# Expert slots that are given out 0.7 of a step later from the fourth group on

## The chip, the cores and the metric

The kernel runs on one core of a Trainium2 chip. The metric is the time of one execution on the device in microseconds (us). Before the change four runs gave 1210.75 to 1219.62 us, with a median of 1216.89 us.

## What is computed

The input is four images of 256 channels and 64 x 64 pixels, in 32-bit floats. Layer 0 is a local attention (each pixel looks at its 3 x 3 neighbours) behind a group norm and an instance norm. Layer 1 treats each pixel as a token: a windowed attention over 64 tokens, then a mixture of eight experts in which every token goes to two of them.

```python
# layer 0
x = x + _L0_conv_ref(_gn(x), ...)
# layer 1: tokens
t = _to_tokens(x)
t = t + _L1_attn_ref(_ln_t(t), Wp, bp, Wg)
t = t + _L1_ffn_ref(_ln_t(t), router_w, w1, b1, w2, b2)
...
    rw, re = jax.lax.top_k(probs, 2)
    for e in range(8):
        h = gelu(tokens @ w1[e] + b1[e])
        out = out + combine[:, e:e + 1] * (h @ w2[e] + b2[e])
```

## The kernel before

**Blocks and steps.** The 16,384 tokens are cut into NB = 32 blocks of 512. The main loop runs over steps g = 0 to 33. A step works on several blocks at once, each at another stage: attend(g) is the second half of the local attention, tail(g-1) the windowed attention and the router of the block before, ranks(g-2) finds the place of every token of the block before that in its expert's list, and produce(g+1) starts the next block. These four are generators. The loop goes round them and takes one piece of each in turn. A step has about 27 pieces, and after each of them follow(g + n/27) is called.

**Rows.** For each of a block's four tiles of 128 tokens and each of a token's two choices, ranks queues one indirect transfer that scatters the rows to the DRAM buffer `rows_in` by expert (L1001, on POOL's queue, 256 in all). They wait in the list `waiting` until give_rows hands them out: two or four with each slot's sum, and all that are left of a group just before a slot of that group is fetched.

**Groups and slots.** The first 28 blocks form 15 groups: 13 of two blocks and two of one. (The last four blocks are handled apart, in `halves` and `together`.) When a group's last block has been ranked, the group's slots are known: a slot is 256 rows of one expert. There are 105 slots. Group 0 has 1, the groups of two have 8 each, the groups of one have 4 each, so `first_slot` is 0, 1, 9, 17, ..., 97, 101, 105.

**One slot** (generator `experts`): a fetch of 272 KB from `rows_in` on SP's queue (L1171, tile sx, 8 buffers); a copy of the expert's first weights on ACT (L1188); four transposes on PE (L1195) and a copy of their result on ACT (L1199); eight matmuls (L1207), and two Gelu on ACT (L1213); eight matmuls (L1225), and two additions and two products on DVE (L1229, L1230); two indirect transfers on POOL's queue that add the rows to `out` (L1244). The parts of one slot are spread over the generator's turns: a slot is fetched two slots ahead of its transposes. Each slot takes four turns.

**What sets the order.** follow(at) decides how many turns of `experts` stand behind each piece of the blocks' work. It takes the smaller of two broken lines over the step number `at`. `most` says how many slots may have been given out: it passes through the points (begins[k], first_slot[k] - 3), where begins[k] is the moment at which the first slot of group k may be fetched. `wanted` is a straight line that spreads the slots evenly: from 1 slot at 6.35 to 94 at step 32, which is 3.63 slots a step. Where `most` is the smaller, eight slots go to two steps, so 4 a step.

The framework that lowers the program keeps close to this order, though it can put an instruction earlier: the first fetch (L1171) is issued at 121.9 us, in step 4, while the lines ask for the first slot after 6.35.

**Ramp and end.** Before step 4 no rows are there, so there are no slots. For blocks below RAMP = 7 the token rows are scaled on ACT, later on DVE. The last four blocks' experts run behind step 33, in smaller units.

Of the kernel before, what the change touches and what calls it, by code (L numbers as in the profile page):

```python
# [62 lines left out]
def hybrid_block_kernel(ctx: ExitStack, tc: tile.TileContext, ins: dict, out: bass.AP):  # L63
# [29 lines left out]
    NS = NB - 4  # L93
    GROUPS = (*[2] * 13, *[1] * 2)
    assert sum(GROUPS) == NS
    first_of = [sum(GROUPS[:k]) for k in range(len(GROUPS))]
# [1361 lines left out]


    STEPS, LAG = {NB: 17, NB + 1: 12}, 0.35  # L1460
    begins = [at + 2 + LAG for n, at in enumerate(first_of[1:])] + [NS + 2.0]
    most = [(at, max(0, n - FETCH - 1)) for at, n in zip((*begins, NB + 2.0), (*first_slot, first_slot[-1]))]
    wanted = [(begins[1], 1), *((NB + n, first_slot[-1] - m) for n, m in ((0, 11), (1, 7), (2, 3)))]
    stream, done = experts(), 0
# [17 lines left out]
    for g in range(NB + 2):  # L1482
# [10 lines left out]
        n = 0  # L1493
# [75 lines left out]
```

## Time and profile before

| | |
|---|---|
| runs | 1210.75 to 1219.62 us, median 1216.89 |
| profiled execution, its own time | 1213.42 us |
| its span, first to last instruction | 1211.7 us |
| TensorE clock granted, mean | 0.975 |
| DVE busy | 916.5 us, 76% |
| ACT busy | 856.6 us, 71% |
| POOL busy | 702.4 us, 58% |

A block's step is taken here to end with the second of its two sums after the output projection (L738, DVE). In the timeline these ends lie at:

| step | ends at, us | length, us |
|---|---|---|
| 5 | 158.0 | 25.2 |
| 6 | 185.3 | 27.3 |
| 7 | 212.6 | 27.3 |
| 8 | 242.4 | 29.8 |
| 9 | 275.1 | 32.7 |
| 12 | 373.4 | 32.8 (mean of steps 9 to 12) |
| 14 | 441.1 | |
| 20 | 631.2 | 31.7 (mean of steps 15 to 20) |
| 22 | 695.6 | |
| 29 | 919.3 | 32.0 (mean of steps 23 to 29) |
| 31 | 977.5 | |

Steps 13 and 21 (38.2 and 35.7 us) also hold the norm of a new image.

PE is TensorE's matmuls and PEld its weight loads, DVE is VectorE, ACT ScalarE, POOL GpSimd, SP SyncE, which issues the plain DMAs. "PE 32.70 (x263)" in a view by windows reads: busy for 32.70 us in this stretch, with 263 matmul instructions. In a list of waits, each line has the engine and line that waited, what it waited for, and then the total in us, how often, and the longest.

### The profile page before, as it was taken

What the parts mean: (1) busy time and instruction counts of PE and PEld (TensorE: products, weight loads), DVE (VectorE), ACT (ScalarE), POOL (GpSimd) and SP (SyncE); (2) the same over time, 40 slices, a digit from 0 to 9 for tenths busy, and PEclk for the clock granted to TensorE, in tenths of its full rate; (3) what the DMA queues carried; (4) which work ended last, traced back from release to release, by engine and by line L of the source; (5) the groups of instructions that cost most, each with busy time, mean ns of one, the idle gap of its engine ahead of it and who ended that gap; (6) DMA issues with size and microseconds to landing.
All of it is one profiled execution on the core that took longest, in us unless ns stands there. A gap on an engine that the chain in (4) does not pass through costs nothing. (4 is left out here: it accounts for less than half of the span.)

```text
span 1211.7 us, 29026 instructions
## 1 busy us (share of the span) xinstructions
PE 1108.0 (91%) x8762; PEld 791.9 (65%) x8762; DVE 916.5 (76%) x4632; ACT 856.6 (71%) x1752; POOL 702.4 (58%) x642
## 2 busy tenths in 40 slices
PE   5989889999999999999999999999999999868890
PEld 4545456677776766776677766766766677757780
DVE  4588878888898888888888887888878889324344
ACT  1466769788888788777787787877787766436660
POOL 3114226566665667566664756666565767577772
PEclk9999999999999999999999999999999999979995
DMA  9885547776768677777676777677665445845556
GB/s 286 270 305 175 177 136 239 207 177 164 185 178 182 167 210 184 187 201 207 164 174 153 181 188 174 176 175 172 150 167 122 100 104 113 198 88 127 139 124 238
DMA packets 136145, 214.00 MB, mean 177 GB/s; under 512 B 16368, under 2 KB 102400, under 8 KB 131768
## 3 DMA queue, kind: packets, MB, share of 16 engines
q1 hardware_dynamic: 86264, 137.00, 37.2%
q0 software_dynamic: 48352, 73.05, 29.3%
q10 hardware_dynamic: 1376, 2.10, 0.5%
q8 instruction: 73, 1.20, 0.4%
q14 instruction: 80, 0.66, 0.2%
HBM read 120.78 MB, written 91.31 MB: 175 GB/s over the span
## 5 line engine op out<-in xcount | busy, mean ns | idle before, releaser
L1244 POOL DMA_INDIRECT out<-sx x210 | 335.3, 1597 | 212.8 <-issue 40.3
L1001 POOL DMA_INDIRECT rows_in<-tok,rows x256 | 254.7, 995 | 185.6 <-issue 71.6
L1225 PE MATMUL psy<-w,h 128*128 x840 | 213.3, 385 | 0.8 <-issue 0.8
L1207 PE MATMUL psh<-xc,w1s 128*128 128x256 f32 x840 | 204.7, 385 | 0.0
L1225 PEld LDWEIGHTS psy<-w,h 128*128 128x128 f32 x840 | 152.7, 190 | 51.3 <-issue 26.2
L1207 PEld LDWEIGHTS psh<-xc,w1s 128*128 128x128 f32 x840 | 152.5, 191 | 34.5 <-issue 10.4
L576 PE MATMUL psq<-x,qks 128*128 128x512 f32 x256 | 125.4, 612 | 1.8 <-ACT qks L497 1.8
L734 PE MATMUL pso<-mixT,vo 128*128 128x512 f32 x256 | 123.4, 605 | 0.0
L1229 DVE TENSOR_TENSOR sx<-psy,b2b 128x256 f32<-128x256 f32 x210 | 87.7, 418 | 45.8 <-PE psy L1225 41.0
L1213 ACT ACTIVATE h<-psh,w1s 128x256 f32<-128x256 f32 x210 | 88.2, 472 | 31.0 <-PE psh L1207 30.1
L1199 ACT COPY xc<-ptx 128x512 f32<-128x512 f32 x105 | 61.2, 583 | 27.1 <-PE ptx L1195 26.6
L1230 DVE TENSOR_SCALAR sx<-sx 128x256 f32<-128x256 f32 x210 | 77.0, 367 | 2.1 <-DVE sx L1229 0.2
L1213 ACT ACT_TABLE_LOAD x59 | 75.7, 1283 | 0.8
L893 ACT ACTIVATE x<-x,scale 128x256 f32<-128x256 f32 x120 | 63.2, 591 | 18.2 <-DVE scale L867 17.6
L584 ACT ACTIVATE q<-psq,qbb,irc 128x512 f32<-128x512 f32 x64 | 50.0, 781 | 34.4 <-PE psq L576 27.9
L1195 PE MATMUL ptx<-ident,sx 128*128 128x128 f32 x420 | 65.2, 277 | 7.6 <-DMA sx<-rows_in 7.6
L1195 PEld LDWEIGHTS ptx<-ident,sx 128*128 128x128 f32 x420 | 50.5, 144 | 32.4 <-issue 15.9
L780 PE MATMUL psp<-wpr,x1c 128*128 128x136 f32 x512 | 70.3, 282 | 0.4 <-DVE ispread L473 0.4
L576 PEld LDWEIGHTS psq<-x,qks 128*128 128x128 f32 x256 | 46.2, 195 | 35.6 <-issue 34.6
L780 PEld LDWEIGHTS psp<-wpr,x1c 128*128 128x128 f32 x512 | 65.6, 190 | 4.5 <-issue 2.1
L734 PEld LDWEIGHTS pso<-mixT,vo 128*128 128x128 f32 x256 | 45.5, 190 | 34.3 <-issue 30.1
L832 PE MATMUL psw<-wl,bandl 128*64 128x512 f32 x128 | 67.0, 635 | 0.0
(277 smaller groups left out, 2501.2 us busy)
## 6 DMA issues: line engine op xcount, KB each, us to landing
xp<-in_xp SPq DMA_DIRECT2D x32, 1024.0 KB
sx<-rows_in SPq DMA_DIRECT2D x105, 272.0 KB
x<-in_x SPq DMA_DIRECT2D x32, 660.0 KB
xs<-in_xs SPq DMA_DIRECT2D x32, 512.0 KB
out<-x SPq DMA_DIRECT2D x28, 512.0 KB
sxa<-rows_in SPq DMA_DIRECT2D x32, 136.0 KB
rows_in<-tok,rows POOLq DMA_INDIRECT x256
out<-sx POOLq DMA_INDIRECT x210
```

The costliest lines, as they stand in the source:

```text
L576: inst = nc.tensor.matmul(ps.rearrange("p (r w) -> p r w", w=W), qks[:, ci, co * P : (co + 1) * P], t[:, ci, 1 : TH + 1, 1 : W + 1], start ...
L734: nc.tensor.matmul(ps, vo[:, ci, co * P : (co + 1) * P], mixT[:, ci, :], start=(ci == 0), stop=(ci == NC - 1),)
L780: nc.tensor.matmul(ps[:, u, :], xc[:, ci, t * P : (t + 1) * P], wpr[:, ci, :], start=(ci == 0), stop=(ci == NC - 1),)
L832: one = nc.tensor.matmul(to[0:WIN], bandl, wl[part], start=True, stop=True)
L1001: return nc.gpsimd.indirect_dma_start(out=rows_in[:, :], out_offset=bass.IndirectOffsetOnAxis(ap=rows[:, c, t : t + 1], axis=0), in_=tok[: ...
L1195: nc.tensor.transpose(pt[:, c, t * P : (t + 1) * P], xs[:, t, c * P : (c + 1) * P], ident)
L1207: nc.tensor.matmul(ps[:, f, :], w1s[:, o : o + P], xc[:, ci, :], start=(ci == 0), stop=(ci == NC - 1),)
L1213: inst = nc.scalar.activation(h[:, f, :], ps[:, f, :], AF.Gelu, bias=w1s[:, F1 + f : F1 + f + 1])
L1225: nc.tensor.matmul(ps, h[:, f, t * P : (t + 1) * P], w2[:, e, f, :], start=(f == 0), stop=(f == NC - 1),)
L1229: nc.vector.tensor_add(ys[:, t, :], ps, b2b[:, e, :])
L1230: nc.vector.tensor_scalar_mul(ys[:, t, :], ys[:, t, :], xs[:, t, bass.ds(e + C, 1)])
L1244: inst = nc.gpsimd.indirect_dma_start(out=out, out_offset=bass.IndirectOffsetOnAxis(ap=xs[:, t, C + E : C + E + 1].bitcast(U32), axis=0), ...
```

## The change

`begins` is computed in another way. Nothing else is touched.

```diff
     STEPS, LAG = {NB: 17, NB + 1: 12}, 0.35
-    begins = [at + 2 + LAG for n, at in enumerate(first_of[1:])] + [NS + 2.0]
+    begins = [at + 2 + min(LAG * max(n, 1), 1.05) for n, at in enumerate(first_of[1:])] + [NS + 3.0]
     most = [(at, max(0, n - FETCH - 1)) for at, n in zip((*begins, NB + 2.0), (*first_slot, first_slot[-1]))]
     wanted = [(begins[1], 1), *((NB + n, first_slot[-1] - m) for n, m in ((0, 11), (1, 7), (2, 3)))]
```

first_of[k] is the first block of group k: 0, 2, 4, ..., 24, 26, 27. The points of `most` move as follows:

| group | first fetch, step, before | after |
|---|---|---|
| 0 | 4.35 | 4.35 |
| 1 | 6.35 | 6.35 |
| 2 | 8.35 | 8.70 |
| 3 | 10.35 | 11.05 |
| 4 | 12.35 | 13.05 |
| 5 to 12 | 14.35 to 28.35 | 0.70 later each |
| 13 | 29.35 | 30.05 |
| 14 | 30.0 | 31.0 |

`wanted` starts at begins[1], which is 6.35 in both.

## The prediction

> **What bounds the kernel now.** I read the page first: its sums, then PE in 40 slices of some 30 us each, about one slice to a step.
>
> ```profile
> PE 1108.0 (91%) x8762; PEld 791.9 (65%) x8762; DVE 916.5 (76%) x4632; ACT 856.6 (71%) x1752; POOL 702.4 (58%) x642
> ...
> PE   5989889999999999999999999999999999868890
> ```
>
> PE has no slack in the middle. The windows by step say where it has some: steps "4 and 5" together, then 6, 7 and 8 alone, then three long stretches without an image norm.
>
> ```profile
> 109.00:158.00 49.00, 40.25 (x394) 22.78 (x394) 41.15 (x258) 32.27 (x74) 17.47 (x22) 0.93 0.53 171
> 158.00:185.30 27.30, 23.32 (x207) 14.90 (x208) 19.77 (x124) 19.68 (x42) 8.73 (x10) 0.94 0.42 141
> 185.30:212.60 27.30, 26.46 (x228) 17.51 (x227) 24.51 (x145) 26.97 (x52) 16.16 (x16) 1.00 0.83 250
> 212.60:242.40 29.80, 29.80 (x248) 20.70 (x247) 25.10 (x126) 23.68 (x50) 16.65 (x14) 1.00 0.75 205
> 242.40:373.40 131.00, 130.82 (x1042) 93.85 (x1041) 111.92 (x564) 110.16 (x207) 83.06 (x69) 1.00 0.70 176
> 441.10:631.20 190.10, 188.59 (x1517) 132.05 (x1516) 162.11 (x831) 151.38 (x294) 124.00 (x103) 1.00 0.75 192
> 695.60:919.30 223.70, 222.06 (x1780) 155.72 (x1779) 184.52 (x983) 174.99 (x343) 141.18 (x117) 1.00 0.69 172
> ```
>
> The columns after the length are PE, PEld, DVE, ACT, POOL, then the clock. In step 6 PE is idle for 4.0 us, in step 7 for 0.8 (there ACT is busy for 26.97 of 27.3 us), and from step 8 on for less than 1% of the time. So from step 8 on the end is set by the sum of PE's work, and the order of the work costs only what it makes PE wait.
>
> What a slot costs PE I take from starts, as busy times overlap. The timeline of PE in step 8 to 9 has a whole slot's three parts in a row:
>
> ```profile
> 241.47 0.60 PE L1195 MATMUL ptx<-ident,sx 128*128 128x128 f32 x4
> 241.91 1.89 PE L1207 MATMUL psh<-xc,w1s 128*128 128x256 f32 x8
> 243.64 1.89 PE L1225 MATMUL psy<-w,h 128*128 x8
> 245.36 0.60 PE L1195 MATMUL ptx<-ident,sx 128*128 128x128 f32 x4
> ```
>
> From 241.47 to 245.36 is 3.89 us a slot. The first stretch (steps 9 to 12) holds 128 of the eight-a-slot matmuls L1225, so 16 slots: 131.0 - 16 x 3.89 = 68.8, or 17.2 us a step for the blocks' own work. Steps 15 to 20 hold 176, so 22 slots: 190.1 - 85.6 = 104.5, or 17.4 a step. Steps 23 to 29 hold 208, so 26: 223.7 - 101.1 = 122.6, or 17.5 a step. Four slots to every step is 0.2 to 0.3 us a step better than an uneven 3.6 or 3.7.
>
> Last, the waits of SP for scattered rows, because that is what an early fetch must meet. The first line below is of the list of SP's waits from 213 to 412 us, the second from 412 to 700, the third of SP's timeline.
>
> ```profile
> SPq L1171 <- DMA rows_in<-tok,rows: 45.1, 4, 17.3
> ...
> SPq L1171 <- DMA rows_in<-tok,rows: 29.4, 4, 14.0
> ...
> 250.85 13.45 SPq L1171 DMA_DIRECT2D sx<-rows_in  x3
> ```
>
> From 700 to 978 us there is no such wait. SP stands for 74.5 us, but PE doesn't: its waits for sx between 133 and 978 us are 4.8 us in all, and both lie before 213.
>
> **What the change moves.** No instruction is added or removed. Putting numbers into the two lines of the code, the slots due are:
>
> at step 7: 1.95 before, 1.66 after; at 8: 4.95, 4.21; at 9: 8.60, 7.02; at 10: 12.60, 10.43; at 11: 16.60, 13.83; from 11.05 to 14.35 2.80 fewer; at 17: 39.61, 37.80; at 20: 50.49, 49.80; from 22 on the same.
>
> Before, `most` is the lower line until 14.35, at 4 slots a step, and `wanted` after it at 3.63. After, `most` rules until about 21.7: 2.55 slots a step up to 8.70, 3.40 up to 11.05, then 4. The last points (31.0 for 30.0) never decide: at 30 `wanted` is 86.75 and `most` 94 or more. So the change is this: up to 2.80 slots are taken out of steps 6 to 10 and put back in steps 14 to 21. Groups 0 and 1 start as before, and the last ten steps and the end behind step 33 get the same order.
>
> **Step by step.** A moved slot takes everything along. PE: 3.89 us. ACT: the weights' copy 0.627, the copy of the transposes 0.583, two Gelu of 0.472, and 12 table loads of 1.283 in the 16 slots of 242 to 373 us, 0.96 each; 3.1 us in all. DVE: 2 x (0.418 + 0.367) = 1.57. POOL: two sums of 1.597 and the up to four row transfers of 0.995 that it hands out. SP: the fetch (272 KB, 0.38 us to issue). On SP's queue the fetch falls behind the loads of x, of the patches and of the statistics and the store of that part of the step, which thus go earlier; on POOL's the sums and rows fall behind the rim copies (0.84).
>
> 1. Slots leave step 6: 0.29 x 3.89 = 1.1 us of PE work. Step 6 is not set by PE (23.32 of 27.3), so I refund nothing: +1.1. The bounds: 0, if it shortens by as much, and 0.74 x 3.89 = 2.9, if step 7, which loses 0.45 slot more, doesn't shorten either. I take 1.1, as step 7 is full on ACT and 0.45 x 3.1 us of that leave too.
> 2. Slots leave steps 8 to 10: 2.77 - 0.74 = 2.03 slots. PE is full there, so they shorten by 2.03 x 3.89 = 7.9, as long as nothing else becomes the limit. DVE is the next: 25.10 of 29.8 in step 8, less 0.84 x 1.57. With 2.9 slots step 8 would have 17.2 + 11.3 = 28.5 against 23.8 on DVE: it stays PE's. An uneven 3.4 costs 0.25 a step more: +0.75.
> 3. The 2.8 slots come back in steps 14 to 21, 10.9 us, which cancels the 7.9 and what left steps 6 and 7. Eight steps go to an even 4: 8 x -0.25 = -2.0. The bounds of this evenness: 0, if it is chance, and the ceiling worked out in the first rival.
> 4. The fetch of a group's first slots comes 0.7 step, some 23 us, after the old place; the longest wait for rows was 17.3 us. So most of SP's 74.5 us vanish. What hides them now is the lead of two slots (half a step, 16 us) between fetch and transposes, with PE waiting for none of it after 213 us. I cost it at 0. What SP meets next is its wait for a free sx buffer (140.8 us from 412 to 700), which PE doesn't see either. If the cover failed, one late fetch would cost PE up to 17.3 - 16 = 1.3 us, eight of them 10.
>
> Sum: 1.1 + 0.75 - 2.0 + 0 = -0.2 us on the profiled execution's 1213.4 (its span is 1211.7, with 1.7 outside). That one lies 3.5 us under the median of the runs, 1216.9; so about 1216.5 for the median.
>
> [...] The view of PE in step 6 has this:
>
> ```profile
> 164.79 2.12 PE L780 MATMUL psp<-wpr,x1c 128*128 128x136 f32 x16
> 170.84 0.33 PE L1195 MATMUL ptx<-ident,sx 128*128 128x128 f32 x1 [3.93 <-DMA sx<-rows_in]
> 171.01 3.00 PE L576 MATMUL psq<-x,qks 128*128 128x512 f32 x4
> ```
>
> After 3.93 us without work four matmuls took 3.00 us that take 1.89 at 252.97, and the step's clock was 0.94: 0.06 x 27.3 = 1.6 us lost. From 185 us to 887 the clock is 1.00. [...]
>
> **The rivals.**
>
> *Faster: the middle has hidden waits, and the early fetches made them.* The blocks' own PE work in step 9, start to start, is 16.4 us (psw 2.0, ptp 0.2, ptx 0.9, psq 3.5, psr 0.6, psc 1.0, psp 1.9, ptm 0.9, psk 0.4, pss and psb 1.4, pso 3.5). Against 17.2 to 17.5 that leaves 0.8 to 1.1 us a step that could go, 15 us over steps 8 to 22, and 4.8 in steps 6 and 7. If half of the 15 went, it would be -7.5: 1209. For: SP's 74.5 us of waits sit in exactly these steps, and hold back the loads queued behind. Against: steps 23 to 29, which have none of these waits, are no better (17.5).
>
> *Slower: the ramp has a floor.* If steps 6 to 10 are held by the blocks' own chain of stages and not by PE, removing slots returns nothing, and they are paid in full later: 2.77 x 3.89 = 10.8, so up to 1227.7; with two thirds, about 1224. It decides from 1.6 slots on that aren't refunded (6.1 us). For: steps without any slot still take 24.5 us (49.0 for two), and three-slot steps later 30.2 to 30.5. Against: PE is busy for all of step 8's 29.80.
>
> *It doesn't do what it says.* If the framework reorders by readiness, the new points hardly move the instructions, and the time is 1216.9.
>
> **How the numbers follow.** About 0.5% (6 us) is what a measurement of this kernel can tell from no change. No difference beyond that, my forecast with the third rival in it: 0.46, its own range 1211 to 1222. Faster 0.26, at 1204 to 1210. Slower 0.28, at 1223 to 1230. The likeliest is 1216.5. The range, 1206 to 1227, leaves out the outer parts of both.
>
> **What would show it.** Right: fetches (L1171) of slots 9 to 50 up to 0.7 step later against the blocks; SP's waits for rows_in in 213 to 700 us well under 30 us; steps 8 to 10 shorter by about 2 us or more each, steps 14 to 21 longer by about 1.4 each; step 22 to the end as long as before, so that all of the difference lies before step 22. Wrong: PE idle for more than 2 us in steps 7 or 8, or a clock under 1.00 there (the floor); or blocks' own work of under 17 us a step (the hidden waits); or a changed end behind step 31, for which I have no reason.

## The result, and the profile after

The changed kernel takes 1220.51 us (median of 52 runs, 1213.49 to 1228.51) against 1214.18 for the kernel before (78 runs). The ratio is 1.0050, with a 95% interval of 1.0038 to 1.0061: slower by 0.5%, some 6 us. The profiled execution has a span of 1212.1 us against 1211.7, but its first steps happened to be quicker: step 5 ends at 152.7 us instead of 158.0, before any moved slot. So I compare from there. From the end of step 5 to the last instruction it is 1059.4 us after, 1053.7 before: 5.7 us more, which fits the runs.

The page after, its sums and PE in 40 slices:

```profile
PE 1103.1 (91%) x8762; PEld 789.2 (65%) x8762; DVE 916.4 (76%) x4632; ACT 840.0 (69%) x1740; POOL 702.0 (58%) x642
...
PE   5988889999999999999999999999999999859890
```

PE has the same work (8762 matmuls). ACT has 12 instructions fewer (1740 against 1752), all of them table loads: the new order needs 53 for Gelu and 25 for Exp (L634), where the old one needed 59 and 31. So the prediction's "No instruction is added or removed" isn't quite true, and the kernel is slower though ACT has less to do. Nothing in the slices tells where 6 us went. Three windows do: steps 6 to 11, steps 12 to 22, and the rest. First before, then after:

```profile
158.00:340.60 182.60, 177.60 (x1459) 123.60 (x1460) 152.71 (x817) 152.09 (x296) 103.13 (x88) 0.99 0.70 190
340.60:695.60 355.00, 352.72 (x2858) 249.41 (x2857) 301.54 (x1557) 283.60 (x548) 226.15 (x190) 1.00 0.73 180
695.60:1211.70 516.10, 450.81 (x3227) 343.44 (x3225) 348.66 (x1655) 337.74 (x712) 330.11 (x268) 0.95 0.62 151
```

```profile
152.70:327.50 174.80, 167.81 (x1401) 113.45 (x1402) 146.21 (x803) 136.81 (x276) 96.75 (x85) 0.99 0.68 192
327.50:696.90 369.40, 365.10 (x2916) 260.99 (x2915) 307.55 (x1571) 282.05 (x555) 232.46 (x195) 1.00 0.72 178
696.90:1212.10 515.20, 449.02 (x3227) 341.51 (x3225) 349.02 (x1655) 337.80 (x712) 329.75 (x267) 0.96 0.62 150
```

The columns are length, PE, PEld, DVE, ACT, POOL, clock, DMA share and GB/s. Steps 6 to 11 got 7.8 us shorter, steps 12 to 22 got 14.4 longer, and behind step 22 the time is 0.9 us shorter. To see what that means, the slots' own PE work has to come off. By starts, a slot's parts cost 4 x 0.11 us (L1195), 1.73 (L1207, eight) and 1.72 (L1225, eight). Steps 6 to 11 hold 80, 155 and 144 of these matmuls before (73.3 us) and 68, 133 and 120 after (62.0): 11.3 us of work left, and the time fell by 7.8. Steps 12 to 22 hold 164, 328 and 328 before (159.5 us), and 176, 350 and 352 after (170.7): 11.2 us of work came, and 14.4 us of time. The blocks' own time, which is what remains, went from 109.3 to 112.7 us in steps 6 to 11 and from 195.6 to 198.7 in 12 to 22. The loss is in two places, about 3 us in each.

In the first place the steps 6 to 10, one line each, answer to the rows of 6, 7 and 8 shown before:

```profile
152.70:180.20 27.50, 23.39 (x207) 14.91 (x208) 19.81 (x124) 19.72 (x42) 8.75 (x10) 0.94 0.41 140
180.20:206.00 25.80, 24.44 (x218) 15.89 (x217) 22.45 (x126) 23.13 (x47) 13.82 (x13) 1.00 0.85 261
206.00:234.00 28.00, 27.76 (x232) 18.05 (x231) 24.48 (x136) 23.89 (x49) 16.66 (x16) 1.00 0.64 190
234.00:264.40 30.40, 30.40 (x250) 21.29 (x249) 26.87 (x152) 21.08 (x44) 19.57 (x16) 1.00 0.76 194
264.40:296.40 32.00, 30.72 (x250) 21.35 (x249) 26.58 (x131) 27.72 (x52) 17.92 (x16) 1.00 0.70 191
```

Step 8 fell from 29.8 to 28.0 us, but 2.8 us of slot work had left it; step 10 fell by only 0.6 us (from 32.5), and PE is idle there for 1.3. In the second place the steps come in pairs. The windows of steps 15 to 18 after:

```profile
428.80:461.80 33.00, 33.00 (x262) 23.39 (x261) 27.41 (x144) 24.13 (x49) 22.37 (x18) 1.00 0.71 175
461.80:495.50 33.70, 32.74 (x262) 23.56 (x261) 27.35 (x136) 26.43 (x52) 19.68 (x17) 1.00 0.75 194
495.50:528.50 33.00, 33.00 (x262) 23.39 (x261) 27.48 (x146) 23.89 (x48) 20.81 (x18) 1.00 0.71 169
528.50:562.30 33.80, 32.78 (x262) 23.62 (x261) 27.39 (x136) 26.51 (x52) 19.12 (x16) 1.00 0.73 186
```

All four hold the same work (262 matmuls), but every second one is 0.7 to 0.8 us longer, with PE idle for 1.0. Before, the four-slot steps 9 to 12 took 32.5 to 32.9 us each. The timeline of PE in step 16 shows what it waits for, and that of ACT why it comes late:

```profile
466.43 1.89 PE L1225 MATMUL psy<-w,h 128*128 x8
469.28 0.25 PE L832 MATMUL psg<-wl,bandl 128*64 128x36 f32 x1 [0.96 <-ACT wl L824]
```

```profile
462.54 0.85 ACT L823 COPY wl<-wx 64x795 f32<-64x795 f32 x1 [3.42 <-DVE wx L811]
463.40 1.28 ACT L1213 ACT_TABLE_LOAD   x1
464.69 0.84 ACT L1213 ACTIVATE h<-psh,w1s 128x256 f32<-128x256 f32 x2
465.55 1.28 ACT L634 ACT_TABLE_LOAD   x1
...
468.17 1.06 ACT L824 COPY wl<-wx 64x1060 f32<-64x1060 f32 x1
```

The tile wl feeds the first matmul of the windowed attention (L832), which needs both copies, L823 and L824. Between them on ACT's queue stand a slot's Gelu and the Exp (L634) of the softmax of the block two later, each with a table load of 1.28 us ahead of it: 4.8 us from the end of the first copy to the start of the second. The copies of the same block (14) in the kernel before, in ACT's timeline at the end of step 15:

```profile
471.64 0.85 ACT L823 COPY wl<-wx 64x795 f32<-64x795 f32 x1 [1.16 <-DVE wx L811]
472.51 1.08 ACT L824 COPY wl<-wx 64x1060 f32<-64x1060 f32 x1
473.60 1.28 ACT L634 ACT_TABLE_LOAD   x1
```

The copies stand together, and the table load behind them. In the built order of ACT's queue an Exp stands between the two copies in blocks 8, 9, 10, 14, 16 and 18 after, and of all these in none before. PE waits in five of the six, not in block 9, where the copies are 3.3 us apart. Only one of the five waits, 0.9 us in step 10, lies in steps 6 to 11; the others are in steps 12, 16, 18 and 20. The lists of PE's waits from 213 to 640 us, after and then before:

```profile
PE psg L832 <- ACT wl L824: 4.8, 5, 1.0
```

```profile
PE psg L832 <- ACT wl L824: 0.5, 1, 0.5
```

SP's waits for scattered rows did go. In the list of SP's waits from 213 to 412 us after there is this line where 45.1 us stood, and from 412 to 700 us none where 29.4 stood:

```profile
SPq L1171 <- DMA rows_in<-tok,rows: 5.4, 1, 5.4
```

### The profile page after: what moved, and what is told of

Read it like the earlier page. It is cut to its first block, busy times and chain, and to the rows that moved or that the text cites. A ratio compares the mean times of both kernels' runs of the same rounds, so it can differ in the third digit from the quotient of the medians.

```text
span 1212.1 us, 29008 instructions
## 1 busy us (share of the span) xinstructions
PE 1103.1 (91%) x8762; PEld 789.2 (65%) x8762; DVE 916.4 (76%) x4632; ACT 840.0 (69%) x1740; POOL 702.0 (58%) x642
## 5 line engine op out<-in xcount | busy, mean ns | idle before, releaser
L1244 POOL DMA_INDIRECT out<-sx x210 | 334.5, 1593 | 197.9 <-issue 29.0
L1225 PE MATMUL psy<-w,h 128*128 x840 | 215.5, 386 | 0.2
L1207 PE MATMUL psh<-xc,w1s 128*128 128x256 f32 x840 | 204.9, 385 | 0.6 <-DVE sx L1229 0.6
L1225 PEld LDWEIGHTS psy<-w,h 128*128 128x128 f32 x840 | 151.8, 190 | 48.6 <-issue 24.0
L1207 PEld LDWEIGHTS psh<-xc,w1s 128*128 128x128 f32 x840 | 152.7, 191 | 36.4 <-issue 13.1
L1195 PE MATMUL ptx<-ident,sx 128*128 128x128 f32 x420 | 64.4, 275 | 6.3 <-DMA sx<-rows_in 6.3
L823 ACT COPY wl<-wx 64x795 f32<-64x795 f32 x32 | 27.3, 852 | 60.5 <-DVE wx L811 60.4
L1195 PEld LDWEIGHTS ptx<-ident,sx 128*128 128x128 f32 x420 | 50.7, 142 | 27.2 <-issue 12.0
```

Source lines behind the costliest of these rows:

```text
L1195: nc.tensor.transpose(pt[:, c, t * P : (t + 1) * P], xs[:, t, c * P : (c + 1) * P], ident)
L1207: nc.tensor.matmul(ps[:, f, :], w1s[:, o : o + P], xc[:, ci, :], start=(ci == 0), stop=(ci == NC - 1),)
L1225: nc.tensor.matmul(ps, h[:, f, t * P : (t + 1) * P], w2[:, e, f, :], start=(f == 0), stop=(f == NC - 1),)
L1244: inst = nc.gpsimd.indirect_dma_start(out=out, out_offset=bass.IndirectOffsetOnAxis(ap=xs[:, t, C + E : C + E + 1].bitcast(U32), axis=0), ...
```

## The experiments

Two theories. **Theory 1**: the loss is the wait for wl, made by the order that the new points give ACT's queue. **Theory 2**: it is the slots; taken from the ramp they are not refunded in full, and they cost their full price later.

All ratios are against the kernel before, run beside them on the same chip.

**The copies first.** In one pair of kernels the copies to wl get the scheduler's first priority, on the changed kernel (after_wl_first) and on the one before (before_wl_first).

```diff
-        nc.scalar.copy(wl[WIN:P, 1:NT, :], wx[WIN:P, 0 : NT - 1, :])
-        pace(nc.scalar.copy(wl[0:WIN], wx[0:WIN]))
+        at, tc.cur_priority = tc.cur_priority, 0 if g >= RAMP else tc.cur_priority; nc.scalar.copy(wl[WIN:P, 1:NT, :], wx[WIN:P, 0 : NT - 1, :])
+        pace(nc.scalar.copy(wl[0:WIN], wx[0:WIN])); tc.cur_priority = at
```

> The changed kernel, with one thing more: the two copies to wl on ScalarE (L823, L824) get the scheduler's first priority from block 7 on, so that no Exp (L634) and no table load stands between them on ScalarE's queue. The changed kernel has such an Exp in between in six blocks (8, 9, 10, 14, 16, 18), and TensorE waits about 1 us for L824 there. Theory 1 (the loss is this wait, made by the order on ScalarE): the 4 to 6 us come back, ratio to the kernel before 1.000 to 1.002, no wait of psg for wl of 0.9 us or more between 213 and 640 us, steps 16, 18 and 20 at 33.0 us like 15, 17 and 19. Theory 2 (slots taken from the ramp are not refunded, and the fuller steps later cost their full price): ratio stays at 1.004 to 1.006.

> The control: the kernel before, with the same first priority for the two copies to wl (L823, L824). It has no Exp between them but at block 28. Both theories: 0.999 to 1.001. If it were 0.996 or less, the copies' priority would be a gain of its own, and what it gives the changed kernel would not tell of the change.

Measured: 0.9986 (0.9959 to 1.0013) and 0.9985 (0.9956 to 1.0014). The loss is gone, and the control hardly gains. PE's list of waits from 213 to 640 us in after_wl_first has no wait for wl left; its longest line is this:

```profile
PE ptm L721 <- ACT mix L711: 0.3, 1, 0.3
```

By the runs that speaks for theory 1. The trace says less. The blocks' own time is 111.8 us in steps 6 to 11 and 197.9 in 12 to 22: 4.8 us over the kernel before, where the changed kernel had 6.5. Another 2.6 us were won in steps 23 to 31; the control wins 3.3 us there in this profile, and 1.6 when it is profiled again (before_wl_third).

The control also shows how far one profile can be trusted. No slot moved in it, and yet its own time is 109.7 and 198.7 us, so 3.5 us over the kernel before, with 4.4 us more in step 21 alone, which holds the norm of an image. So the 3 us of steps 12 to 22 can't be told from one profile. Steps 14 to 20, which hold no norm, are steadier: 122.6 us before and 124.8 after; with the copies first 121.1 (control), 121.8 (before_wl_third) and 123.3 (after_wl_first).

**One half of the move alone.** late_only (the first line) and early_only (the other two) change only `begins`:

```diff
+    begins = [at + 2 + (LAG if n < 4 else 1.05) for n, at in enumerate(first_of[1:])] + [NS + 3.0]
...
+    lags = {2: 0.70, 3: 1.05, 4: 0.85, 5: 0.60}
+    begins = [at + 2 + lags.get(n, LAG) for n, at in enumerate(first_of[1:])] + [NS + 2.0]
```

> The points of most stay as before for groups 0 to 3 and lie 0.7 of a step later from group 4 on, so that steps 6 to 10 get the slots that they had and the 2.8 slots are taken from steps 10 to 12 instead. On ScalarE an Exp stands between the two copies to wl in four blocks (11, 14, 16, 18). Theory 1: 4 waits of about 1 us, ratio 1.003 to 1.004. Theory 2 (the ramp): ratio 1.000 to 1.001, as TensorE was full in steps 10 to 12 and refunds what is taken.

> The points of groups 2 and 3 lie later as in the change (0.35 and 0.70 of a step), then come back: 0.50 later for group 4, 0.25 for group 5, as before from group 6 on. The 2.8 slots are taken from steps 6 to 10 and put back in steps 11 to 16. An Exp stands between the copies to wl in four blocks (8, 9, 10, 14), in three of them while TensorE is already full. Theory 1: ratio 1.002 to 1.003. Theory 2: the ramp's share, some 3.5 us, ratio 1.003, and in steps 17 to 21 nothing against the kernel before. The two differ in where it is lost: theory 1 in waits for wl, theory 2 in steps 6 to 9 that stay long with fewer slots.

Measured: late_only 0.9997 (0.9973 to 1.0021), early_only 1.0035 (1.0010 to 1.0061). late_only has four Exp in between and waits for wl 2.9 us between 213 and 640 us, and theory 1 asked for 1.003 to 1.004 of it: a miss for theory 1 alone. The own time of steps 6 to 11 is 109.6 us in late_only, as before, and 113.5 in early_only. By the runs theory 2 fits this pair. The trace of late_only does show its waits: the own time of steps 14 to 20, where all of them lie, is 126.4 us, against 122.6 before.

**Twice the move, and the pair again.** double_wl_first takes `1.05 if n == 2 else 1.75` from group 2 on, late_wl_first is late_only with the copies first, and the pair of the first experiment ran once more beside them.

> On the kernel before with the copies to wl first: the points of most for group 2 lie 0.70 and from group 3 on 1.40 of a step later, twice the change. Up to 5.6 slots leave steps 6 to 10. With no waits for wl, theory 1 (the waits alone) gives the same as before_wl_first, 0.998 to 1.001. Theory 2 (slots that leave the ramp are not refunded; 2.5 us of the changed kernel's loss without the waits) gives twice 2.5, so 5 us over before_wl_first, 1.003 to 1.005 against the kernel before.

> late_only with the copies to wl first: steps 6 to 10 as before, slots later from group 4 on, no Exp between the copies. Theory 1 and theory 2 both: as before_wl_first, 0.997 to 1.000. If it is over 1.002, there is a cost in the fuller steps 13 to 21 which neither names.

> after_wl_first once more, beside before_wl_first on one chip, for a narrower interval. Theory 1: the two agree within 0.1%. Theory 2: this one is 0.2 to 0.3% (2.5 to 3.5 us) slower than before_wl_first, but faster than the changed kernel's 1.005.

> before_wl_first once more: 0.997 to 1.000 against the kernel before by both theories. In the last profile its steps 23 to 31 took 3.3 us less than before and one step (21) 4.4 us more, with a dip of the clock: if that dip is not there again, 0.996 to 0.998.

These four came to a chip on which everything took longer, the kernel before 1270.65 us; the ratios are within that chip. Measured: 1.0097 (1.0063 to 1.0130), 0.9997 (0.9963 to 1.0031), 0.9990 (0.9957 to 1.0022) and 0.9984 (0.9945 to 1.0023). So with the copies first, 2.8 slots later cost nothing that the runs can tell, and 5.6 slots later cost 1.1% over the control. Theory 1 can't explain the second, theory 2 not the first, if its cost is in proportion.

**The wait without the move.** behind_six and behind_twelve leave every slot where it was before, and put the second copy behind the Exp by an order alone:

```diff
-            nc.scalar.activation(
+            exps[g] = nc.scalar.activation(
                 pe[:, n, 0:NKEY], s[:, n], AF.Exp, bias=top[:, n : n + 1],
...
-        pace(nc.scalar.copy(wl[0:WIN], wx[0:WIN]))
+        pace(inst := nc.scalar.copy(wl[0:WIN], wx[0:WIN])); g in (8, 9, 10, 14, 16, 18) and after(inst, exps[g + 2], "behind the softmax")
```

behind_twelve has range(8, 20). three_slots is the changed kernel with 1.10 for 1.05, and after_beside the changed kernel itself.

> The kernel before, points of most and all, but in the six blocks 8, 9, 10, 14, 16 and 18 the second copy to wl (L824) is put behind the Exp (L634) on ScalarE's queue, as it stands in the changed kernel. No slot is moved. Theory 1 (the loss is this order): six waits of TensorE of about 1 us, ratio 1.004 to 1.005. Theory 2 (it is the slots): 1.000 to 1.001.

> The same for blocks 8 to 19; the Exp then stands between the copies in 11 of them. Theory 1: twice as many waits, ratio 1.007 to 1.010. Theory 2: 1.000 to 1.002.

> The changed kernel with 1.10 in place of 1.05: from group 3 on the points lie 0.75 of a step, so three whole slots, later, instead of 0.70. Slots leave the ramp as in the change (0.2 more). ScalarE's order has an Exp between the copies in blocks 8, 9 and 10 alone; in 14, 16 and 18 a copy of transposes stands there instead. Theory 1: about half of the loss, 1.002 to 1.003. Theory 2: 1.005 to 1.006.

> The changed kernel itself beside these three on one chip, so that they can be compared with it directly: 1.004 to 1.006 by both theories.

Measured: behind_six 1.0019 (0.9993 to 1.0045), behind_twelve 1.0038 (1.0015 to 1.0061), three_slots 1.0073 (1.0046 to 1.0100), after_beside 1.0062 (1.0042 to 1.0082). PE's waits from 213 to 640 us in behind_six and then in behind_twelve:

```profile
PE psg L832 <- ACT wl L824: 2.5, 4, 0.8
```

```profile
PE psg L832 <- ACT wl L824: 5.6, 8, 1.0
```

The order alone costs time, without any slot moved: behind_twelve shows it, while the interval of behind_six reaches 1. 0.38% over 11 blocks is 0.4 us a block, so 2.5 us for six. That is less than half of the changed kernel's loss, and half of what theory 1 foretold. But these kernels wait less in a block than the changed one, so a price by blocks is too low for it. Over the 0.5 us of the kernel before, behind_six waits for wl 2.0 us more and loses 2.3; behind_twelve waits 8.2 us more, with one wait of 3.1 us at 647 us, just behind this window, and loses 4.6. At these two prices the changed kernel's 4.3 us more would cost 2.4 to 4.9 us, an estimate from two ratios with intervals of over 0.2%.

three_slots shows the other side: its steps 14 to 20 hold no Exp in between, and their own time is 121.3 us, under the 122.6 of the kernel before and the 124.8 of the changed one. But it is no faster, as steps 6 to 11 cost 113.2 us all the same, and in step 21 PE stood for 2.4 us for the new image's norm.

**The rest.** What stayed open was the ramp without waits:

> early_only with the copies to wl first: slots leave steps 6 to 10 as in the change and come back in steps 11 to 16, and nothing on ScalarE stands between the copies. If the ramp has a cost of its own: 2.5 to 3.5 us over before_wl_first (beside it in this call), mostly in steps 7 to 10. If not: the same as before_wl_first within 0.1%.

> double_wl_first once more, on a chip with the usual times if it comes to one: 5.6 slots taken instead of 2.8. A ramp cost in proportion gives 5 to 7 us over before_wl_first; the 14 us of the first time would mean that more slots taken are refunded less and less.

> The reverse, with the copies to wl first: from group 2 on the points lie 0.25 of a step earlier than before, one slot. If the ramp's filling is what counts, up to 1 us under before_wl_first, as TensorE has 0.8 us left in step 7; if fetches too early cost, it is slower by SP's waits for rows, which can be over 16 us long here and reach TensorE: 1 to 4 us.

> before_wl_first beside these three, as what they are compared with: 0.998 to 1.000 against the kernel before.

Measured: early_wl_first 1.0007 (0.9986 to 1.0028), double_wl_again 1.0098 (1.0071 to 1.0125), lag10_wl_first 0.9989 (0.9964 to 1.0013), before_wl_third 0.9983 (0.9959 to 1.0007). early_wl_first lies 0.24% (2.9 us) over its control, as asked for, but with intervals of 0.2% on both it is not shown by the runs. The traces are steadier than the runs, as the own time of steps 6 to 11 comes out alike wherever the ramp is alike (us, from profiles of the usual chips):

| ramp as before | | slots taken from steps 6 to 10 | |
|---|---|---|---|
| before | 109.3 | after, after_beside | 112.7, 114.2 |
| late_only | 109.6 | three_slots | 113.2 |
| behind_six, behind_twelve | 109.4, 109.9 | early_only | 113.5 |
| before_wl_first, before_wl_third | 109.7, 109.5 | after_wl_first, early_wl_first (no waits for wl) | 111.8, 112.6 |
| lag10_wl_first (one slot earlier) | 110.0 | double_wl_again (5.6 slots, 0.7 us of waits for wl) | 115.5 |

The four kernels in the right column that aren't marked have 0.8 to 0.9 us of waits for wl in these steps. So, against the 109.3 to 109.7 us of the kernel before and its control, 2.8 slots taken leave 2.1 to 3.3 us unrefunded where no wait for wl is in it, and 5.6 slots leave 5.8 to 6.2, 0.7 of it this wait: about 1 us a slot, in proportion. double_wl_again loses the rest of its 14 us later: the own time of steps 12 to 22 is 207.1 us against 196.3 in before_wl_third, with 4.1 us of waits for the image norm in steps 13 and 21 among it.

The reverse wins nothing beyond the control. The copies first on the kernel before are at 0.9985, 0.9984 and 0.9983 on three chips, each interval reaching 1: perhaps 0.15% better than the kernel before, not shown.

## Why the prediction was wrong

The forecast was no change, 1216.5 us by a sum of -0.2. The time, 1220.51 us, lies in the range, and even in the own range of "no difference", but that is luck of the base: the four runs behind 1216.9 lay 2.7 us above the median of 78. As a difference, -0.2 us was said and +6.3 measured, a loss of 0.5%, clear of noise. The sum has no term for a wait of PE that the new order makes on ACT's queue, and it has one for evenness that isn't there. Step by step:

- **Step 3 failed**, "Eight steps go to an even 4: 8 x -0.25 = -2.0". The own time of steps 14 to 21 went up by 2.3 us (141.74 to 144.08), not down by 2.0. No run shows a gain from evenness: in steps 14 to 20 the uneven slots have 121.1 and 121.8 us with the copies first, the even ones 123.3 with the copies first and 121.3 in three_slots, where no Exp stands between. What the place of the slots did change is ACT's queue: 0.7 of a step later, it gets an Exp and two table loads between the copies to wl in every second step (blocks 14, 16 and 18, and 8 and 10 before them; in block 9 it is an Exp and one load). PE's waits for wl went from 0.5 to 4.8 us, 4.3 more, of which 3.4 lie in steps 12 to 20. behind_twelve (1.0038) shows that such an order costs time with no slot moved, and three_slots, 0.05 of a step further on, is without it in blocks 14, 16 and 18.
- **Step 2 failed in part**, "PE is full there, so they shorten by 2.03 x 3.89 = 7.9" less 0.75 for unevenness. The own time of steps 8 to 10 rose by 2.8 us (51.2 to 54.0) instead of 0.75. 0.9 us is the wait for wl in step 10; the rest is what taken slots leave unrefunded. That PE was busy for all of 29.80 us didn't mean that work taken out comes back at its price: in step 8 after, 1.0 us of the 2.8 that left wasn't returned, though PE is idle for only 0.2. Why not is open; that the slots had covered waits which then came out would explain it, but no run shows it.
- **Step 1 held in its size, not in its place**: +1.1 was said, and the own time of steps 6 and 7 rose by 0.7. But step 6, as measured, holds the same slot matmuls after as before (207 in both lines); 2.0 us of slot work left step 7, and it shortened by 1.5.
- **Step 4 held**: SP's waits for rows fell from 74.5 to 5.4 us, and nothing came of it: PE's waits for sx between 133 and 978 us were 4.8 us before and are 4.7 after.
- **The last points** (31.0 for 30.0) decide nothing: with either, the smaller of the two lines is the same at every step number. From step 23 on there was nothing to lose, and nothing was lost (0.9 us less).
- **Two readings of the lines** were off by little: before, `most` rises by 3 slots a step up to 8.35, not by 4, and after, it rules until 21.85, not 21.7. The slots due that the sum rests on come out as said.
- **The clock** took no part in the ramp's loss: from step 7 on the steps of the ramp have a clock of 1.00 after as before, and step 6 has 0.94 in both.
- **The rivals**: the floor was the nearest. It was priced at up to 10.8 us and is worth some 2 to 3. Its signs didn't come (PE is idle for 1.4 us in step 7 and 0.2 in step 8, at a clock of 1.00), so whether the blocks' chain holds those steps isn't shown. The rest of the loss is a mechanism that I hadn't named, though ACT's order around the copies could be seen in the trace of before.

Two mechanisms together, then: 2.4 to 4.9 us from ACT's order (an estimate; that such an order costs time with no slot moved is shown in behind_twelve, by 0.38%), and 2 to 3 us from the ramp (shown in the traces of all kernels that take slots there, and by runs with the copies first only for twice the move). In the trace of the changed kernel they add up: 4.3 us more of waits for wl and some 2.5 of ramp without them make 6.8, and the own time rose by 6.5. By this, taking the waits away should leave some 2.5 us, 0.2%, over the control. The runs gave 0.9986 against 0.9985 and 0.9990 against 0.9984, so less, though the intervals of 0.3% hold both: how much of the ramp's share the runs have stays open.

## What to carry to other kernels

When work is moved in a schedule that another program lowers, the cost need not lie in the amount moved alone. Here some of it, 2.4 to 4.9 us by the estimate above, lay in what ACT's queue then had in front of the next thing that PE needed: a Gelu, an Exp and two table loads of 1.28 us between the copies that fill one tile, so that PE, the busiest engine (91%), waited for the second copy for up to 1.0 us. So compare the queues' order around the chain that feeds the busiest engine. Nor did an engine that was busy for all of a step (PE in step 8, 29.80 of 29.80 us) refund the work that was taken out at its price: of 2.8 us, 1.8 came back. And a difference of 0.2 to 0.3 us a step between the means of a few stretches is no price until a run has varied it alone.

## What the runs showed that I hadn't expected

- In 14 profiles (usual chips) whose instructions are the same up to there, step 5 ended between 152.7 and 161.1 us. That is as large as the effect studied, so profiles were compared from there on.
- One chip of the same type ran the kernel before in 1270.65 us instead of 1215, 4.5% more, with the granted clock of its profiles at 0.970 to 0.975, within what the others have (0.967 to 0.980).
- The step of a new image's norm is the least steady: step 21 took 35.7 us before and 43.6 in early_wl_first, with the same slots in it. PE waited for 5.8 us for the norm's first matmul there, in its list of waits from 360 to 720 us:

```profile
PE gm L469 <- ACT x L768: 5.8, 1, 5.8
```
